# A Mamba-attention-MoE block on one core: first attention group fed from SBUF, pairwise maxima, warm-up products and a shorter spread of side work

## The chip, the core and the metric

The kernel runs on one core of one Trainium2 chip. Its time is device time in microseconds; the time before is the median of three runs. Engines are named as in the profile: PE is TensorE (matrix products), DVE VectorE, ACT ScalarE, POOL GpSimd, SP the engine that issues most transfers.

## The reference, cut to what matters

```python
x = L0_attn_x                                  # (8, 512, 256)
xn = _layernorm(x, axis=-1)
x = x + _L0_attn_ref(xn, ...) + _L0_ffn_ref(xn, ...)

# _L0_attn_ref: projection, causal convolution over 4 rows, a linear state-space scan
# with 16 states, silu, output projection
u = x @ W_in + b_in
u = conv(u, conv_w) + conv_b
h = At @ h + u_t * Bp ; y_t = Cp . h + Dp * u_t
return silu(y) @ W_out + b_out

# _L0_ffn_ref: attention of 16 heads of width 16, and a mixture of 8 experts, top 2
qkv = (x @ W_qkv + b_qkv).reshape(B, S, 3, H, hd)
attn = softmax(q k^T / sqrt(hd)) @ v
gate = softmax(x @ W_gate + b_gate); top_g, top_i = top_k(gate, 2)
moe_out = sum over the two experts of gate * (x @ W_experts[e] + b_experts[e])
return attn_out + moe_out
```

## The kernel before

Rows of one batch (512) lie in four tiles of 128. Attention runs in 32 groups: 8 batches times 4 groups of four heads. A group `i` has eight steps `s`, each one tile `t` of 128 rows times one pair `pr` of heads (`t, pr = divmod(s, 2)`), so there are 256 steps in all. A step number in the text counts them: step 8 i + s.

For each half `h` of a batch's heads, `project_ops` makes queries (w = 0) and keys (w = 1): PE multiplies (`on_pe`, 16 instructions through `mm2`, line 132), ACT rounds the result to the fast matrix format (`upper`, line 1397), DVE makes the remainder (`lower`, line 1402), and SP stores both parts to DRAM (`store`, line 1413). `load_stack` then fills `qs` and `ks` for one group with 16 transfers of 64 KB issued by SP (line 1434), in which the parts are repeated so that one product holds the sum over parts.

A group then goes through `maxima` (PE, line 1443) and `reduce_max` (DVE, line 1455), once for each of the eight steps; `place_parts` (DVE), `place_turn` (PE) and `place_row` (ACT) turn the maxima into a row `mrow`; `weights` (PE, lines 1479 and 1487) makes scores less maximum, `exponent` (ACT, line 1497) the exponentials, `values` (PE, line 1506) multiplies with the values, and `norm_evict`, `norm_turn`, `norm_scale`, `norm_add` divide by the sums and add to `acc` on POOL (line 1537).

Side work goes on between these steps: `gates_of` (layer norm, transposes, gates), `v_of` (values), `scan_setup` (the scan as a convolution kernel), `route_ops` and `scatter_ops` (routing; POOL writes rows by index, line 1076), `ssm_ops` (scan `ps_zx`, projection `ps_z` line 1279, convolution on DVE line 1294, output `ps_o` line 1317), `moe_ops` (36 blocks of 256 rows, products `ps_e`, result to `y_d`), and `combine_ops` (POOL gathers two expert rows per token, 64 gathers at line 1157, and adds them, line 1167).

The order of all instructions comes from a planner in the kernel itself. `op(engine, us, at, fn, needs, makes, takes, frees, ...)` enters an operation with its assumed cost and a due time `at` in steps. `plan` is a greedy list scheduler: on each engine it takes the operation that can start first, or among those within 0.2 us the one that is marked `first` or due earliest. `takes` and `frees` name buffers with a number of copies (`rings`); PSUM has three pairs `m` and one single `m1`. `run_all` makes six plans and emits the shortest by the planner's own count. Each engine then runs its instructions in that fixed order, so one instruction that waits holds up all behind it on the same engine. `needs` like `reach(at)` only order the plan; on the chip only the data and the buffers are waited for.

The due times of the side work come from `spread`, which lays the sum `SIDE` of its costs evenly over the steps from -`LEAD` to the last step:

```python
    def spread(ws):
        for w in ws:
            total[0] += w
            yield -LEAD + (NK - 1 + LEAD) * (total[0] - w / 2) / SIDE
```

with `NK` = 256 and `LEAD` = 6. Transfers that are not needed at once (`later`: W_in, W_out, the biases) are planned after the stack of group 1.

## Time and profile before

| what | before |
|---|---|
| median of three runs | 826.58 us (825.75 to 827.12) |
| profiled execution | 856.68 us |
| its span | 855.0 us |
| PE busy | 761.3 us, 89% |
| DVE busy | 558.9 us, 65% |
| ACT busy | 477.4 us, 56% |
| POOL busy | 387.8 us, 45% |
| moved by DMA | 148.69 MB, 174 GB/s |
| granted PE clock, mean | 0.963 |

The times of single instructions all come from the one profiled execution, which took 30 us longer than the median; its sum is compared with 856.68, not with 826.58. A row of the profile names the line of the kernel, the engine, what is written and read, how often, busy time and the mean of one, and in brackets or behind the bar how long the engine stood idle before it and what ended the wait. "issue" is time for which the profile shows no cause. A row of the windows gives busy time in a stretch for each engine, the number of instructions, the granted PE clock, and the share of the DMA engines. In the chain by time each line is a piece of the chain that ended last: start, length, what.

### The profile page before, as it was taken

To read this page: it belongs to the slowest core of one execution; us is meant where nothing else is said; L and a number is where in the kernel's file an instruction comes from. 1 tells how busy PE (TensorE), PEld (TensorE's weight loads), DVE (VectorE), ACT (ScalarE), POOL (GpSimd) and SP (SyncE) were. 2 spreads that over 40 slices of the span, in tenths; PEclk is the share of its full clock that TensorE was granted. 3 is DMA by queue.
4 is the path that set the end of the run, shared out by engine and by line. 5 is a ranking of instruction groups with operands and counts; after the bars stand their busy time and mean duration, and the time that the engine had idled before them with its cause. 6 is when DMAs were issued, how large, how long until landed. Compare 5 with 4: busy or idle time off the path is not lost.

```text
span 855.0 us, 15265 instructions
## 1 busy us (share of the span) xinstructions
PE 761.3 (89%) x5788; PEld 452.5 (53%) x5788; DVE 558.9 (65%) x852; ACT 477.4 (56%) x652; POOL 387.8 (45%) x419
## 2 busy tenths in 40 slices
PE   4887888988787888999999999999999979897996
PEld 3643454644344445467666676666566645453543
DVE  2466777799773474973547874534885636956884
ACT  2345677444874476854655755665664645535552
POOL 4001011797656755453323322322222145888884
PEclk9998999998988899999999999999999999998999
DMA  6567777332673545477877674897565772969231
GB/s 140 174 178 207 206 221 202 121 75 73 209 205 131 190 131 173 139 209 248 205 212 241 172 226 143 252 234 219 143 172 162 216 191 75 242 177 221 78 108 38
DMA packets 110412, 148.69 MB, mean 174 GB/s; under 512 B 33883, under 2 KB 70787, under 8 KB 110340
## 3 DMA queue, kind: packets, MB, share of 16 engines
q1 hardware_dynamic: 94212, 96.33, 41.0%
q0 software_dynamic: 16128, 51.39, 20.4%
q8 instruction: 46, 0.75, 0.4%
q14 instruction: 26, 0.21, 0.1%
HBM read 96.28 MB, written 51.38 MB: 173 GB/s over the span
## 4 chain that ended last, share of the span: by engine, by line
PE 53%; POOL 16%; DVE 12%; ACT 7%; issue 6%; DMA 4%; another core or an unknown queue 1%; SPq 1%; POOLq 0%; ACTq 0%; DVEq 0%
PE av L1506 8%; PE ps_e L132 8%; POOL got L1157 7%; PE ps_qk L132 6%; DVE mx L1455 5%; PE ps_mx L1443 5%; PE ps_p L1479 5%; PE ps_o L1317 5%; POOL res L1167 5%; PE ps_z L1279 4%; PE ps_p L1487 4%; ACT p L1497 4%; PE ps_zx L132 2%; PE ps_v L132 2%; POOL acc L1167 2%
## 5 line engine op out<-in xcount | busy, mean ns | idle before, releaser
L1455 DVE TENSOR_REDUCE mx<-ps_mx 128x2 f32<-128x1024 f32 x256 | 312.0, 1220 | 166.1 <-PE ps_mx L1443 131.8
L1497 ACT ACTIVATE p<-ps_p 128x1024 f32<-128x1024 f32 x256 | 257.6, 1023 | 117.6 <-PE ps_p L1487 89.2
L1443 PE MATMUL ps_mx<-ks,qs 64*128 64x512 f32 x512 | 126.2, 483 | 23.6 <-DVE mx L1455 19.6
L1479 PE MATMUL ps_p<-qs,ks 64*128 64x512 f32 x512 | 125.1, 483 | 18.5 <-ACT p L1497 11.5
L1506 PE MATMUL av<-p,v_aug 128*32 128x512 f32 x1024 | 127.4, 608 | 0.5 <-issue 0.4
L1487 PE MATMUL ps_p<-mrow,pick 64*128 64x512 f32 x512 | 106.7, 411 | 0.2 <-ACT mrow L1473 0.2
L1443 PEld LDWEIGHTS ps_mx<-ks,qs 64*128 64x128 f32 x512 | 51.4, 190 | 90.9 <-DVE mx L1455 37.4
L1479 PEld LDWEIGHTS ps_p<-qs,ks 64*128 64x128 f32 x512 | 51.1, 195 | 82.3 <-ACT p L1497 28.2
L1111 POOL DMA_DIRECT2D xg<-xs_d x36 | 47.2, 1311 | 95.3 <-PE ps_xg L137 40.8
L1537 POOL TENSOR_TENSOR acc<-acc,attn 128x256 f32<-128x256 f32 x32 | 24.9, 778 | 141.3 <-DVE attn L1530 126.3
L1076 POOL DMA_INDIRECT xs_d<-xs,slot x64 | 65.9, 1030 | 49.2 <-ACT xs L1092 34.1
L1294 DVE SCALAR_TENSOR_TENSOR ys<-th,cw,ys 128x511 f32<-128x511 f32 (+2 forms) x96 | 78.4, 816 | 1.7
L1157 POOL DMA_INDIRECT got<-y_d,slot x64 | 64.8, 1013 | 25.0 <-issue 15.3
L132 PE MATMUL ps_e<-wt,xgT 64*128 64x256 f32 x576 | 69.6, 381 | 1.1 <-DMA wt<-in_L_ffn_W_experts_dram,wrow 0.4
L1279 PE MATMUL ps_z<-zx,wi 128*128 128x512 f32 x128 | 65.7, 637 | 2.7 <-DVE acc L1327 2.1
L1116 POOL DMA_INDIRECT wt<-in_L_ffn_W_experts_dram,wrow x36 | 36.4, 1012 | 68.3 <-PE ps_mx L1443 29.8
L1317 PE MATMUL ps_o<-wo,ys 128*128 128x256 f32 x256 | 62.8, 388 | 1.5 <-DVE ys L1308 1.5
L132 PEld LDWEIGHTS ps_e<-wt,xgT 64*128 64x128 f32 x576 | 54.3, 186 | 12.2 <-ACT xgT L1130 4.8
L1506 PEld LDWEIGHTS av<-p,v_aug 128*32 128x32 f32 x1024 | 27.4, 110 | 57.5 <-issue 56.1
L1487 PEld LDWEIGHTS ps_p<-mrow,pick 64*128 64x128 f32 x512 | 52.2, 198 | 5.8 <-issue 0.4
L1317 PEld LDWEIGHTS ps_o<-wo,ys 128*128 128x128 f32 x256 | 47.5, 195 | 7.6 <-DVE ys L1308 2.3
L132 PE MATMUL ps_qk<-xnTr,wqkv_sb 64*128 64x256 f32 x384 | 46.3, 381 | 2.9 <-ACT p L1497 2.8
(188 smaller groups left out, 963.8 us busy)
## 6 DMA issues: line engine op xcount, KB each, us to landing
split<-parts SPq DMA_DIRECT2D x32, 512.0 KB
qs<-split SPq DMA_DIRECT2D x256, 64.0 KB
ks<-split SPq DMA_DIRECT2D x256, 64.0 KB
xg<-xs_d POOLq DMA_DIRECT2D x36, 256.0 KB
y_d<-y SPq DMA_DIRECT2D x36, 256.0 KB
xn_d<-xn SPq DMA_DIRECT2D x32, 128.0 KB
acc<-in_L_attn_x_dram SPq DMA_DIRECT2D x8, 512.0 KB
xnr<-xn_d SPq DMA_DIRECT2D x16, 256.0 KB
```

The costliest lines, as they stand in the source:

```text
L132: mm(o, lhsT=lhs, rhs=rhs, start=(j == 0), stop=(j == len(parts) - 1))
L1076: nc.gpsimd.indirect_dma_start(out=xs_views[view], out_offset=bass.IndirectOffsetOnAxis(ap=index, axis=0), in_=src, in_offset=None,)
L1157: nc.gpsimd.indirect_dma_start(out=got[b, h][:, t, i, :], out_offset=None, in_=y_d[:, :], in_offset=bass.IndirectOffsetOnAxis(ap=slot[:, i ...
L1279: mm(held["z", b, ct], lhsT=wi[:, c, ct * P : (ct + 1) * P], rhs=zx[b][:, c, :], start=(c == 0), stop=(c == ND - 1),)
L1294: nc.vector.scalar_tensor_tensor(y[:, lag:S], held["th", b, ct][:, 0 : S - lag], cw[:, ct, k : k + 1], bias_tab[:, ct, :] if lag == 0 else ...
L1317: mm(o, lhsT=ys[b][:, ct, t * P : (t + 1) * P], rhs=wo[:, ct, :], start=False, stop=(ct == NCT - 1),)
L1443: mm(ps[:, u, :], lhsT=qs[i % 3][64 * u : 64 * u + 64, pr, t * P : (t + 1) * P], rhs=ks[i % 3][64 * u : 64 * u + 64, pr, :], start=True, s ...
L1455: nc.vector.tensor_reduce(mx[i][:, t, 2 * pr : 2 * pr + 2], held["x", i, s], AX.X, ALU.max, negate=True)
L1479: mm(ps[:, u, :], lhsT=ks[i % 3][64 * u : 64 * u + 64, pr, t * P : (t + 1) * P], rhs=qs[i % 3][64 * u : 64 * u + 64, pr, :], start=True, s ...
L1487: mm(ps[:, u, :], lhsT=pick[64 * u : 64 * u + 64, pr, :], rhs=held["mrow", i][64 * u : 64 * u + 64, :], start=False, stop=True,)
L1497: nc.scalar.activation(p, held["s", i, s], AF.Exp, scale=SCALE)
L1506: mm(av[i][j * HW : (j + 1) * HW, :], lhsT=v_aug[b % 2][:, t, o : o + HW], rhs=pm[i, 2 * t + j // 2][:, j % 2, :], start=(t == 0), stop=(t ...
```

## The change

Four edits are made together.

1. For group 0 alone, `qs` and `ks` are filled from the parts in SBUF (`load_first_stack`) rather than from their copy in DRAM, in 32 transfers of 32 KB, one set of 16 for each pair of heads and w: queries issued by SP, keys by ACT (`nc.scalar`). The store of these parts is planned 8 steps later.
2. For group 0 the steps are taken by pairs: first the four with pair 0 (`s` = 0, 2, 4, 6), then those with pair 1. `place_parts`, `place_turn` and `place_row` run once for each pair, into an `mrow` of their own.
3. `warm` puts 40 products of the identity matrix with itself on PE ahead of everything else.
4. `spread` lays the side work over steps up to 250 instead of 255 (`EARLY` = 5).

As the planner makes all orders anew, the instructions of every engine are ordered differently from there on.

```diff
--- before.py
+++ after.py
@@ -560,6 +560,15 @@
     op("pool", 0.8, -4, set_flip, makes=["flip"])
 
 
+
+    def warm():
+        ps = pair("ps_warm")
+        for n in range(40):
+            mm(ps[:, n % 2, 0:P], lhsT=ident, rhs=ident, start=True, stop=True)
+
+    op("pe", 4.0, -99, warm, takes=[("m", "warm")], frees=[("m", "warm")], shape=3)
+
+
     toep = const.tile([P, S], F32, name="toep")
     bias_tab = const.tile([P, NCT, S], F32, name="bias_tab")
     kpad = dram.tile([1, P + S], F32, name="kpad")
@@ -1418,22 +1427,29 @@
         at = 16 * h - 24
         fast = h == 0
         for w in range(2):
-            M, T, R = ("m", "qk", h, w), ("parts", h, w), ("split" + str(w), h)
-            op("pe", 1.75, at, lambda w=w: on_pe(w), needs=xT_keys(b) + ["wqk"], makes=[("qk", h, w)], takes=[M, T, R], frees=[("xnT", b)])
+            M, T, R = ("m", "qk", h, w), ("parts", h, w), [("split" + str(w), h)]
+            op("pe", 1.75, at, lambda w=w: on_pe(w), needs=xT_keys(b) + ["wqk"], makes=[("qk", h, w)], takes=[M, T] + R, frees=[("xnT", b)])
             op("act", 0.69, at, lambda w=w: upper(w), needs=[("qk", h, w), "bqk"], makes=[("up", h, w)], first=True)
             op("dve", 0.75, at, lambda w=w: lower(w), needs=[("up", h, w)], makes=[("lo", h, w)], frees=[M], first=fast)
-            op("sp", 0.4, at + 0.5, lambda w=w: store(w), needs=[("lo", h, w)], makes=[("split", h, w)], frees=[T], kb=512)
+            op("sp", 0.4, at + 0.5 + 8 * fast, lambda w=w: store(w), needs=[("lo", h, w)], makes=[("split", h, w)], frees=[T], kb=512)
 
     def load_stack(i, w):
         st = (qs, ks)[w][i % 3]
-        src = split_of[i // 2, w]
         for u in range(2):
             for r in range(4):
                 part = (r // 2, r % 2)[w]
-                rows = src[part, 4 * HD * (i % 2) : 4 * HD * (i % 2 + 1), :]
-                nc.sync.dma_start(
-                    out=st[64 * u + HD * r : 64 * u + HD * (r + 1), :, :].bitcast(F32),
-                    in_=rows.rearrange("(pr u d) s -> u d pr s", u=2, d=HD)[u],
+                to = st[64 * u + HD * r : 64 * u + HD * (r + 1), :, :].bitcast(F32)
+                rows = split_of[i // 2, w][part, 4 * HD * (i % 2) : 4 * HD * (i % 2 + 1), :]
+                nc.sync.dma_start(out=to, in_=rows.rearrange("(pr u d) s -> u d pr s", u=2, d=HD)[u])
+
+    def load_first_stack(w, pr):
+
+        for u in range(2):
+            for r in range(4):
+                o = (2 * pr + u) * HD
+                (nc.sync, nc.scalar)[w].dma_start(
+                    out=(qs, ks)[w][0][64 * u + HD * r : 64 * u + HD * (r + 1), pr, :].bitcast(F32),
+                    in_=held["pt", 0, w][o : o + HD, (r // 2, r % 2)[w], :].bitcast(F32),
                 )
 
     def maxima(i, s):
@@ -1456,10 +1472,10 @@
             mx[i][:, t, 2 * pr : 2 * pr + 2], held["x", i, s], AX.X, ALU.max, negate=True
         )
 
-    def place_parts(i):
+    def place_parts(i, pairs=slice(0, 2)):
         v = negm[i % 2].rearrange("p t (u c) -> p t u c", u=2)[:, :, :, 0:4]
-        v = v.rearrange("p t u (r z) -> p t u r z", z=2)
-        m = mx[i].rearrange("p t (r u) -> p t u r", u=2)
+        v = v.rearrange("p t u (r z) -> p t u r z", z=2)[:, :, :, pairs]
+        m = mx[i].rearrange("p t (r u) -> p t u r", u=2)[:, :, :, pairs]
         nc.vector.tensor_copy(v[:, :, :, :, 0], m)
         nc.vector.tensor_tensor(v[:, :, :, :, 1], m, v[:, :, :, :, 0].bitcast(F32), ALU.subtract)
 
@@ -1468,9 +1484,11 @@
             f"ps_nm_{i}", [lambda r, t=t: negm[i % 2][r, t, :].bitcast(F32) for t in range(NT)]
         )
 
-    def place_row(i):
-        held["mrow", i] = wk2.tile([P, S], F32R, tag="mrow", name=f"mrow_{i}")
-        nc.scalar.copy(blocks(held["mrow", i]), held["nm", i])
+    def place_row(i, pairs=(0, 1)):
+        row = wk2.tile([P, S], F32R, tag="mrow", name=f"mrow_{i}_{pairs[0]}")
+        nc.scalar.copy(blocks(row), held["nm", i])
+        for pr in pairs:
+            held["mrow", i, pr] = row
 
     def weights(i, s):
         t, pr = divmod(s, 2)
@@ -1487,7 +1505,7 @@
             mm(
                 ps[:, u, :],
                 lhsT=pick[64 * u : 64 * u + 64, pr, :],
-                rhs=held["mrow", i][64 * u : 64 * u + 64, :],
+                rhs=held["mrow", i, pr][64 * u : 64 * u + 64, :],
                 start=False,
                 stop=True,
             )
@@ -1543,36 +1561,65 @@
         K = 8 * i
         Q = [("stack0", i), ("stack1", i)]
         for w in range(2):
+            if i == 0:
+                for pr in range(2):
+                    op(
+                        ("sp", "act")[w], 3.3, K - 16 + 0.1 * w + pr, lambda w=w, pr=pr: load_first_stack(w, pr),
+                        needs=[("lo", 0, w)], makes=[("stack0", w, pr)] + ([("stack", 0, w)] if pr else []),
+                        takes=[] if pr else [("stack" + str(w), 0)], frees=[("parts", 0, w)], kb=256, first=w > 0,
+                    )
+                continue
             op(
                 "sp", 3.6, K - 16 + 0.1 * w, lambda w=w: load_stack(i, w),
                 needs=[("split", i // 2, w), ("split", i // 2, w + i % 2 * (1 - w))], makes=[("stack", i, w)],
                 takes=[("stack" + str(w), i)], frees=[("split" + str(w), i // 2)], kb=512,
             )
-        for s in range(8):
-            k = K + s
-            X = ("m", "mx", i, s)
+
+        turns = ([0, 2, 4, 6], [1, 3, 5, 7]) if i == 0 else (list(range(8)),)
+        n = 0
+        for half, steps in enumerate(turns):
+            for s in steps:
+                k = K + n
+                n += 1
+                X = ("m", "mx", i, s)
+                op(
+                    "pe", 0.24, k - 10, lambda s=s: maxima(i, s), needs=([("stack", i, 0), ("stack", i, 1)] if i else [("stack0", 0, half), ("stack0", 1, half)]) + (reach(k - 18) if i != 1 else [("nm", 0)]),
+                    makes=[("mp", i, s)], takes=[X, ("mx_m", i, s)], first=i == 0,
+                )
+                op(
+                    "dve", 1.23, k - 10, lambda s=s: reduce_max(i, s),
+                    needs=[("mp", i, s)] + ([("mr", i, 0)] if s else []),
+                    makes=[("mr", i, s)], takes=[] if s else [("mx", i)], frees=[X, ("mx_m", i, s)], first=True,
+                )
+            at = K - 2.5 if i else k - 9.5
+            end = half == len(turns) - 1
+            some = slice(half, half + 1) if i == 0 else slice(0, 2)
+            N, R = ("nm", i, half), ("mrow", i, half)
             op(
-                "pe", 0.24, k - 10, lambda s=s: maxima(i, s), needs=[("stack", i, 0), ("stack", i, 1)] + (reach(k - 18) if i != 1 else [("nm", 0)]),
-                makes=[("mp", i, s)], takes=[X, ("mx_m", i, s)],
+                "dve", 0.37, at, lambda some=some: place_parts(i, some), needs=[("mr", i, s) for s in steps] + [("negm0", i % 2)] + ([("nmp", i, 0)] if half else []),
+                makes=[N] + ([("nm", i)] if end else []), takes=[] if half else [("negm", i)], frees=[("mx", i)], first=True,
             )
             op(
-                "dve", 1.23, k - 10, lambda s=s: reduce_max(i, s),
-                needs=[("mp", i, s)] + ([("mr", i, 0)] if s else []),
-                makes=[("mr", i, s)], takes=[] if s else [("mx", i)], frees=[X, ("mx_m", i, s)], first=True,
-            )
-        op(
-            "dve", 0.37, K - 2.5, lambda: place_parts(i), needs=[("mr", i, s) for s in range(8)] + [("negm0", i % 2)],
-            makes=[("nm", i)], takes=[("negm", i)], frees=[("mx", i)], first=True,
-        )
-        op("pe", 0.45, K - 2.5, lambda: place_turn(i), needs=[("nm", i)], makes=[("nmp", i)], takes=[("mt", "nm", i), ("mrow", i)], frees=[("negm", i)])
-        op("act", 0.58, K - 2.5, lambda: place_row(i), needs=[("nmp", i)], makes=[("max", i)], frees=[("mt", "nm", i)], first=True)
-        for s in range(8):
-            k = K + s
+                "pe", 0.45, at, lambda: place_turn(i), needs=[N], makes=[("nmp", i, half)],
+                takes=[("mt", "nm", i, half), R], frees=[("negm", i)], first=i == 0,
+            )
             op(
-                "pe", 0.47, k, lambda s=s: weights(i, s), needs=[("max", i), "pick"], makes=[("wp", i, s)],
-                takes=[("m", "p", i, s), ("p_m", i, s)], frees=Q + [("mrow", i)],
-            )
-            op("act", 1.04, k, lambda s=s: exponent(i, s), needs=[("wp", i, s)], makes=[("p", i, s)], takes=[("p", i, s)], frees=[("m", "p", i, s), ("p_m", i, s)], first=True)
+                "act", 0.58, at, lambda half=half: place_row(i, (half,) if i == 0 else (0, 1)), needs=[("nmp", i, half)],
+                makes=[("max", i, half)] + ([("max", i)] if end else []), frees=[("mt", "nm", i, half)], first=True,
+            )
+        n = 0
+        for half, steps in enumerate(turns):
+            for s in steps:
+                k = K + n
+                n += 1
+                op(
+                    "pe", 0.47, k, lambda s=s: weights(i, s), needs=[("max", i, half), "pick"], makes=[("wp", i, s)],
+                    takes=[("m", "p", i, s), ("p_m", i, s)], frees=Q + [("mrow", i, half)],
+                )
+                op(
+                    "act", 1.04, k, lambda s=s: exponent(i, s), needs=[("wp", i, s)], makes=[("p", i, s)],
+                    takes=[("p", i, s)], frees=[("m", "p", i, s), ("p_m", i, s)], first=True,
+                )
         for hf in range(2):
             vs = [("vd", b, n) for n in range(2)]
             four = [("p", i, s) for s in range(4 * hf, 4 * hf + 4)]
@@ -1605,14 +1652,14 @@
 
     rings["split0"] = rings["split1"] = 2
     NK = B * NG * 8
-    LEAD = 6.0
+    LEAD, EARLY = 6.0, 5.0
     total = [0.0]
 
     def spread(ws):
 
         for w in ws:
             total[0] += w
-            yield -LEAD + (NK - 1 + LEAD) * (total[0] - w / 2) / SIDE
+            yield -LEAD + (NK - 1 - EARLY + LEAD) * (total[0] - w / 2) / SIDE
 
     SSM = [3.9] + [1.75] * 4 + [1.87] * 4 + [0.0]
     SCAN = [0.2] + [0.6] * 9 + [1.0, 1.0, 2.3]
```

## The prediction, made before the changed kernel was run

> **What bounds the kernel now.** I read the page first (busy shares, then the chain that ended last), then the windows, which cut the run into its stages, then the chain by time at the end of the run, and last the timeline of the first 52 us, where most of the edits lie.
>
> ```profile
> span 855.0 us, 15265 instructions
> PE 761.3 (89%) x5788; PEld 452.5 (53%) x5788; DVE 558.9 (65%) x852; ACT 477.4 (56%) x652; POOL 387.8 (45%) x419
> ```
>
> TensorE is busy 89% of the span, so only its idle time (about 94 us) and its slow-clock time can be won. The windows say where these lie:
>
> ```profile
> core 0: us, PE busy (x) PEld busy (x) DVE busy (x) ACT busy (x) POOL busy (x), PEclk, DMA share, GB/s
> 20.00:36.00 16.00, 14.97 (x198) 11.82 (x194) 4.22 (x13) 8.37 (x17) 1.47 (x3) 1.00 0.54 161
> 36.00:51.00 15.00, 10.84 (x66) 7.40 (x62) 11.61 (x15) 1.75 (x3) 0.00 (x0) 0.77 0.84 230
> 380.00:690.00 310.00, 304.77 (x2513) 198.57 (x2513) 184.52 (x249) 178.03 (x238) 84.76 (x79) 1.00 0.72 204
> 735.00:798.00 63.00, 53.41 (x336) 28.08 (x332) 45.17 (x62) 29.82 (x38) 53.71 (x60) 0.92 0.78 204
> 798.00:833.00 35.00, 34.84 (x222) 18.94 (x222) 27.89 (x39) 17.40 (x23) 29.98 (x33) 1.00 0.28 85
> ```
>
> From 380 to 690 PE has 5 us idle in 310: whatever is late there moves the end by the same amount. From 735 to 798 it lacks 9.6 us, and from 798 to 833 almost nothing. Before 36 us it is well filled as well (1.0 us idle in 20 to 36): while the first stack is fetched, PE does the second half's projections and the values of two batches.
>
> ```profile
> 681.32 1.75 PE ps_e L132 x16
> 683.75 5.13 DMA y_d<-y
> 689.15 0.97 POOL got L1157
> ...
> 701.90 9.89 issue
> ...
> 843.64 1.85 issue
> 845.50 0.70 DVE acc L1327
> ```
>
> The end hangs on the last expert product (683), then on a POOL chain of 64 gathers and 64 additions, with a hole of 9.9 us in it, and on PE, whose ps_o ends at 845.4 too. Both tie; cutting one alone gives little.
>
> ```profile
> 13.87 6.52 PE L132 MATMUL ps_qk<-xnT,wqkv_sb 64*128 64x256 f32 x32 [0.68 <-ACT xnT L798]
> 17.71 0.43 DVE L728 BATCH_NORM_STATS2 st<-x 128x6 f32<-128x256 f32 x1 [9.03 <-DMA x<-in_L_attn_x_dram]
> 22.42 4.73 SPq L1434 DMA_DIRECT2D qs<-split  x8
> 23.37 0.59 ACT L892 COPY v_aug<-ps_v 128x512 f32<-128x512 f32 x1 [1.38 <-PE ps_gt L137]
> 36.08 1.15 PE L1443 MATMUL ps_mx<-ks,qs 64*128 64x512 f32 x6
> ```
>
> Here is what the first stack costs now: parts ready at 19.55 and 21.91 (DVE's `lower`), stored, loaded from 22.4 to 30.9 in 16 issues on SP, first maxima at 36.08. From 36 to 51 DVE's eight reductions of 1.22 us set the pace and PE is thin.
>
> **Part 1, identity products (PE, 40 of 128x128).** They run from about 1.5 us (the identity is made by POOL at 1.23 + 0.29) beside the row loads; PE has nothing before 11.77. What they may win is in the row at 13.87: 32 products take 6.52 us where two such sets took 1.89 and 1.95 from 24.99 on, so 2.7 us. The Trainium skill ("TensorE: Matmul & The Clock Gate", What's actually happening) says the clock is halved until PE has been busy for one window of about 3.4 us, which fits, although the window's row shows 1.00 at that time. The same section says that one idle window halves it again, and this speaks against the edit: 40 products at 0.1 to 0.2 us end by 6 to 9.5, before 11.77. By the rule the win is 0 to 2.7 us of PE. I cost it at nothing for another reason, the row at 17.71: `lower` of the queries stands on DVE behind the statistics of batch 1, which wait for a load that lands at 17.7, and the changed DVE order keeps that. `lower` ends at 19.55 and 21.5 instead of 19.55 and 21.91. If the cover were gone it would be 2.7 us.
>
> **Part 2, first stack from SBUF, keys issued by ACT.** Removed from the way to it: the store and the load through DRAM. A DMA issue on SP costs 0.47 us (4 of 8 rows at 0.42 plus 0.047 between). Eight for the query pair 0 run on SP from 19.6 to 23.3, eight for the keys on ACT from 21.5 to 25.3, landing 2.0 us later (a load of 8 KB issued at 12.23 is used at 14.26): first maxima at 27.5, 8.5 us earlier. No row shows a DMA issued by ACT. I take SP's 0.47; the smallest row on SP is 0.22 (be_raw, one row each), so 16 issues cost ACT 3.5 to 7.5 us. The skill ("DMA: Bandwidth & Descriptors", Issuing engines are not separate DMA queues) has the two queues share the same DMA engines and save issue time alone. That is 3.7 us here; the rest of the 8.5 is the DRAM round trip.
> What is queued behind: on ACT both evictions of `ps_v`, then the four normalizations of batch 1 (now 23.4 to 27.5). In the changed order all 16 key issues come first, and the order's waits show that DMAs reuse eight completion semaphores among SP and ACT: the tenth key issue waits for the store of the key parts (512 KB, issued at about 24.2; the query store took 19.58 to 23.9 until the load behind it could go). So ACT comes free at about 28.5 + 7 x 0.47 = 31.8. The second maxima needs the PSUM pair of `ps_v`, so it starts at 32.4, the transposes of batch 1 (after two evictions and 2.1 us of normalization) at 34.5, the gate, the second half's query projection and the rest after that. PE idles from 23.7 to 27.5 and is thin until about 37, and the clock halves, as it did at 40 to 47 now.
> SP: 8 more issues sit between the stores and the second stack, and four stores of normalized rows wait for ACT, so the second stack lands at about 43 instead of 41; it is needed at 50, so this costs nothing. The projection stores of the second half wait for parts that are now made 17 us later; stack 2 lands at about 67 to 69, when it is needed.
>
> **Part 3, maxima by pairs.** Added: two small DVE operations (2 x 0.18), four transposes (0.45), one copy (0.58); 1.4 us in all, off PE but for 0.45. Won: step 0 needs four reductions instead of eight, 4.9 us.
>
> **Front, summed.** I count PE's work in the two instruction orders, each group by its back-to-back row (1.75 for a projection, 0.43 for two 512-wide products, 1.75 for four value pairs, 3.9 for a scan). At step 0 the old order has done 26.9 us, the new one 18.5; at step 8 42.7 and 41.8; at step 16 61.5 and 60.9; at the last expert product 631.3 and 630.9. Step 0 now starts at 50.7, so 23.8 us are lost by then. In the new one, from 34.5 on: gate 1.1, projection 1.75, four more reductions 4.9, place and turn 1.5, second projection 1.75 and maxima between, some at half clock: step 0 at about 48, 29.5 lost. So the first exponentials come some 3 us earlier, with 8 us less work done. Between steps 8 and 16 the old order lets DVE stand 3.5 us for the load of batch 3 (its statistics come after four of eight reductions); the new one puts six before. I give back 3. Front: +3 us (ACT at 0.22 each and no semaphore wait: -5; ACT held longer: +10).
>
> **Part 4, side work five steps shorter.** The order shows what moves: the last batch's scan from step 242 to 236, its first ps_z from 245 to 241, the output products of batch 6 from 243 to 239. Steps 220 to 240 now hold 51.1 us of PE work and will hold 60.6; steps 240 to 250 fall from 32.9 to 23.4. The former ran from 735 to 798 with 9.6 us idle and 5 us lost at half clock; the latter is the full stretch. About half of the moved 9.5 us should fit into waits: -5. The last ps_o waits 1.5 us for DVE (838.65 to 841); with ps_z one step earlier: -1. On POOL the hole of 9.9 goes: attention addition 25 (ready at 711.7) stood ahead of the third group of gathers and now stands behind the fourth, 26 us after the first gather rather than 13. POOL alone would end 10 us earlier, so it no longer ties with PE; worth nothing by itself. Tail: -6 (0 to -10).
>
> **Sum.** 856.7 (span 855.0 and 1.7 around it) + 3 - 6 = 853.7. The reordering of everything between steps 16 and 203 shifts single waits (11 PE gaps of 1.0 to 5.7 us in its timeline there, 22 us in all): 0, with +-4. The median of the runs is 826.6, 3.5% under the profiled execution; I scale the change by 0.965: 823.7 us.
>
> **Rivals.**
> ACT is held too long (slower). Place: the 16 key issues; price: 1 us per us, as transposes, gates and projections are behind them. If the stores take the 6.4 us that one took at 65 and each further semaphore round 2 us more, ACT is free at 38 or later: +10 - 6 = +4, 830.5. It decides from 35 us on, where the sum is zero. For it: PSUM has only three pairs; against: the DMA share of 0.54 leaves room. 0.22.
> The tail gives nothing (slower). ACT stood 6.2 us at 694 to 700 and 4.6 at 775 to 780, each while POOL issued eight gathers in a row. The new order has such a pair in batch 6 instead of batch 4, in the last 50 us, where work was to be fitted in. +3, 829.5; it decides when less than 3 of the 6 arrives. 0.15.
> The front works as meant: ACT issues at 0.22, the store is not waited for: -5 - 6 = -11, 816. For it: first maxima 8.5 us earlier; against: PE had other work then. 0.18.
> The change does nothing in sum, as PE work is the same (777 us): 0.05.
> The sum as written: 0.40.
>
> **The numbers.** Predicted 823.7; its own case spans 819 to 828. The range over the cases is 811 to 835. About 0.2% (1.65 us) is what the measurement tells from no change. Faster: 0.30 of the 0.40 and the 0.18: 0.48. Same: 0.07 of the 0.40 and the 0.05: 0.12. Slower: the two rivals and 0.03: 0.40.
>
> **What would show it.** Right: first maxima at 27 to 28; ACT's first `ps_v` eviction at 31 to 33; first exponential at 47 to 50; step 16 at 93 to 96 (91.7 now); no POOL wait over 3 us after the gathers begin; PE idle between steps 220 and 240 under 6 us. Wrong: the eviction before 27 or after 35; POOL still ending with PE; the last expert product more than 8 us from 683.

## The result, and the profile after

The changed kernel is slower: 833.99 us (median of seven, 829.14 to 840.60) against 826.17 us for the kernel before, a ratio of 1.0093 with a 95% interval of 1.0064 to 1.0122. The forecast was 823.7. The time lies inside the range given, on the other side of no change.

To read the numbers: in some comparisons the kernel before takes about 826 us, in others about 858, and the kernels beside it move with it (some expectations below speak of two chips, but the record has chip 14 at both levels, so the reason is not known); ratios are therefore taken within one comparison, and stages compared between profiles of one level. The profile of before shown above (856.68) and its later repeats are of the 858 level, the profile after (829.14, span 827.4) is of the 826 level. There the kernel with the shorter spread alone (ratio 1.0013 to the kernel before) stands in for the kernel before, which has no profile at that level.

The busy shares of after, and its windows (columns as before):

```profile
span 827.4 us, 15473 instructions
PE 755.2 (91%) x5864; PEld 455.5 (55%) x5864; DVE 555.4 (67%) x854; ACT 475.3 (57%) x653; POOL 391.4 (47%) x419
```

```profile
20.00:36.00 16.00, 7.45 (x38) 5.07 (x39) 4.74 (x10) 2.60 (x6) 1.47 (x3) 0.66 0.45 125
36.00:51.00 15.00, 12.67 (x112) 8.78 (x112) 9.01 (x13) 5.59 (x10) 0.00 (x0) 0.79 0.52 144
380.00:690.00 310.00, 303.48 (x2502) 194.88 (x2498) 183.65 (x246) 178.23 (x240) 94.54 (x91) 1.00 0.72 204
735.00:798.00 63.00, 60.34 (x397) 29.89 (x396) 53.10 (x72) 35.17 (x45) 53.41 (x56) 1.00 0.55 149
```

PE was busy 14.97 of the 16 us from 20 to 36; now it is busy 7.45, at a granted clock of 0.66. The stretch from 380 to 690 is as full as before, so nothing lost ahead of it is made up there. From 735 to 798 the 9.6 us of idle have become 2.7. As the changed kernel is at other steps by then, the same count by steps is safer: from step 220 to 240 PE was idle 9.6 us (8.7 in a later profile) and is now idle 2.8 (4.3 in the second profile), as forecast. The timeline of after, in order of start (start, length, engine, what; in brackets the wait before it):

```profile
1.58 10.71 PE L567 MATMUL ps_warm<-ident 128*128 128x128 f32 x80 [1.58 <-POOL ident masks.py:199]
13.61 3.73 PE L132 MATMUL ps_qk<-xnT,wqkv_sb 64*128 64x256 f32 x32 [0.68 <-ACT xnT L807]
22.33 11.03 ACTq L1450 DMA_DIRECT2D ks<-parts  x15
25.47 6.89 SPq L1450 DMA_DIRECT2D qs<-parts  x8
25.85 0.46 PE L1459 MATMUL ps_mx<-ks,qs 64*128 64x512 f32 x1
30.17 0.76 PE L1459 MATMUL ps_mx<-ks,qs 64*128 64x512 f32 x1 [3.86 <-DMA qs<-parts]
33.40 1.08 ACT L901 COPY v_aug<-ps_v 128x512 f32<-128x512 f32 x2 [14.47 <-DMA ks<-parts]
36.00 1.50 PE L137 MATMUL ps_xT<-ident,xn 64*128 64x64 f32 x16 [1.16 <-ACT xn L754]
48.57 1.02 ACT L1515 ACTIVATE p<-ps_p 128x1024 f32<-128x1024 f32 x1
```

ACT issues keys from 22.33 to 33.36 and does nothing else. What is queued behind, the value evictions, waits until 33.40; PE's maxima need the PSUM pair that they free, and the transposes of batch 1 come at 36.00. The forecast said 31.8 for the end of the issues, 31 to 33 for the eviction, 34.5 for the transposes, and about 48 for step 0. The last part of the chain that ended last is this:

```profile
817.16 0.73 POOL acc L1555
817.89 0.02 issue
817.91 0.70 DVE acc L1336
818.61 0.04 issue
818.65 0.39 PE ps_o L1324
819.04 1.73 PE ps_o L1326 x8
```

POOL's addition releases DVE's, which frees the PSUM pair that PE's last output product needs: in this profile POOL sets the end, and PE waits 2.5 us for it. In the second profile of the same kernel the chain runs through PE, DVE and ACT without POOL from 804 us on, and POOL's last attention addition is itself the one that waits, 4.6 us, for DVE. So the two still tie.

### The profile page after: what moved, and what is told of

The parts are those of the page before. It is cut to its first block, busy times and chain, and to the rows that moved or that the text cites. A ratio compares the mean times of both kernels' runs of the same rounds, so it can differ in the third digit from the quotient of the medians.

```text
span 827.4 us, 15473 instructions
## 1 busy us (share of the span) xinstructions
PE 755.2 (91%) x5864; PEld 455.5 (55%) x5864; DVE 555.4 (67%) x854; ACT 475.3 (57%) x653; POOL 391.4 (47%) x419
## 3 DMA queue, kind: packets, MB, share of 16 engines
q0 software_dynamic: 16128, 51.39, 21.1%
## 4 chain that ended last, share of the span: by engine, by line
PE 51%; DVE 17%; ACT 8%; POOL 7%; DMA 7%; issue 4%; SPq 3%; ACTq 1%; DVEq 0%; POOLq 0%
PE av L1524 8%; PE ps_e L132 7%; DVE mx L1471 7%; PE ps_mx L1459 5%; PE ps_p L1497 5%; PE ps_o L1326 5%; PE ps_qk L132 5%; POOL got L1166 4%; PE ps_p L1505 4%; ACT p L1515 3%; PE ps_z L1288 3%; DVE ys L1303 3%; ACT xs L1101 3%; PE ps_zx L132 2%; DMA got<-y_d,slot 2%
## 5 line engine op out<-in xcount | busy, mean ns | idle before, releaser
L1459 PE MATMUL ps_mx<-ks,qs 64*128 64x512 f32 x512 | 126.0, 478 | 30.9 <-DVE mx L1471 18.0
L1524 PE MATMUL av<-p,v_aug 128*32 128x512 f32 x1024 | 123.5, 600 | 0.0
L1505 PE MATMUL ps_p<-mrow,pick 64*128 64x512 f32 x512 | 104.0, 400 | 0.0
L1459 PEld LDWEIGHTS ps_mx<-ks,qs 64*128 64x128 f32 x512 | 51.1, 189 | 93.5 <-DVE mx L1471 33.9
L1497 PEld LDWEIGHTS ps_p<-qs,ks 64*128 64x128 f32 x512 | 49.9, 189 | 72.9 <-ACT p L1515 25.4
L1166 POOL DMA_INDIRECT got<-y_d,slot x64 | 67.0, 1046 | 24.8 <-issue 14.9
L1326 PE MATMUL ps_o<-wo,ys 128*128 128x256 f32 x256 | 60.4, 379 | 0.0
L132 PE MATMUL ps_qk<-xnTr,wqkv_sb 64*128 64x256 f32 x384 | 49.9, 402 | 3.2 <-ACT p L1515 2.3
```

The costliest lines, as they stand in the source:

```text
L132: mm(o, lhsT=lhs, rhs=rhs, start=(j == 0), stop=(j == len(parts) - 1))
L1166: nc.gpsimd.indirect_dma_start(out=got[b, h][:, t, i, :], out_offset=None, in_=y_d[:, :], in_offset=bass.IndirectOffsetOnAxis(ap=slot[:, i ...
L1326: mm(o, lhsT=ys[b][:, ct, t * P : (t + 1) * P], rhs=wo[:, ct, :], start=False, stop=(ct == NCT - 1),)
L1459: mm(ps[:, u, :], lhsT=qs[i % 3][64 * u : 64 * u + 64, pr, t * P : (t + 1) * P], rhs=ks[i % 3][64 * u : 64 * u + 64, pr, :], start=True, s ...
L1497: mm(ps[:, u, :], lhsT=ks[i % 3][64 * u : 64 * u + 64, pr, t * P : (t + 1) * P], rhs=qs[i % 3][64 * u : 64 * u + 64, pr, :], start=True, s ...
L1505: mm(ps[:, u, :], lhsT=pick[64 * u : 64 * u + 64, pr, :], rhs=held["mrow", i, pr][64 * u : 64 * u + 64, :], start=False, stop=True,)
```

## The experiments

The edits are cut to the lines that matter; lines that only tell the planner the same thing (engine names, keys) are left out. Three theories stood at the start. Theory 1: the front costs (the stack from SBUF, with ACT held), and the loss lasts, as PE is full later. Theory 2: the shorter spread brings nothing or costs. Theory 3: any change makes the planner re-make the order of every engine, and that alone moves the time by several us. "Ratio" is to the kernel before in the same comparison, with its 95% interval. Single executions of one kernel spread by about 1% to either side (the kernel before: 852.11 to 865.07 in 22 runs), so ratios of medians decide and one profile is good for some 5 us.

A measure used below is the time lost at a step: the moment when the step's first exponential starts, minus the PE work that stands ahead of it in PE's instruction order, counted with the same durations as in the prediction. At the end it is the span minus all PE work (777 us). The counted durations are a little too long, so the figure falls where PE is full; only differences between kernels at one level mean something.

| time lost, us, at step | 0 | 8 | 16 | 40 | 80 | 208 | end |
|---|---|---|---|---|---|---|---|
| before (858 level) | 24.8 | 26.9 | 29.8 | 31.0 | 70.5 | 47.4 | 77.2 |
| before + 8 issues on ACT | 29.3 | 31.4 | 33.8 | 34.7 | 72.9 | 51.7 | 76.3 |
| before + 16 issues on ACT | 34.5 | 36.7 | 36.8 | 38.1 | 78.5 | 59.6 | 88.3 |
| before + pairs | 21.4 | 27.1 | 32.5 | 37.8 | 82.5 | 62.2 | 93.8 |
| before + spread (826 level, as all below) | 23.3 | 27.3 | 28.9 | 27.9 | 44.0 | 21.1 | 45.2 |
| after | 30.1 | 32.8 | 33.8 | 33.9 | 55.4 | 35.0 | 50.0 |
| after, second profile | 31.2 | 34.1 | 35.1 | 38.2 | 60.5 | 40.1 | 58.4 |
| after, stack through DRAM | 19.8 | 25.1 | 29.6 | 29.3 | 43.1 | 32.1 | 46.2 |
| after, keys issued by POOL | 21.4 | 29.8 | 30.5 | 31.7 | 56.1 | 34.8 | 51.8 |
| after, keys of pair 1 later | 28.4 | 27.8 | 30.8 | 32.7 | 50.9 | 30.0 | 45.4 |

**Both kernels again.** No edit.

> The kernel before, unchanged: a second profiled execution of it, and how far two sets of runs of one kernel lie apart. All theories: ratio 1.000 within 0.3%. If its profiled span is near 825 and the 380 to 690 stretch ends some 25 to 30 us earlier than in the first profile, the first profile held a disturbance after 260 us and the comparison of stages has to be made with this one.

Measured: 1.0017 (0.9994 to 1.0040), as expected. The profile (span 860.7) is as long as the first one of before (855.0), so that length was no accident of one execution.

> The changed kernel, unchanged, beside the parts below on one chip. Expected: 0.5 to 1.2% slower than the kernel before, as in the first comparison. If it is faster than before by the tail term alone (-0.4% or better), the first comparison turned on the chip.

Measured: 1.0074 (1.0045 to 1.0102), 831.84 against 825.95. The loss repeats.

**One part alone in the kernel before.** First the 40 products:

```diff
+    op("pe", 4.0, -99, warm, takes=[("m", "warm")], frees=[("m", "warm")], shape=3)
```

> Only the 40 identity products are added to the kernel before. If the front is what costs (theory 1: SBUF stack with ACT holding up the second projection) this alone is 0, 825 to 828 us, with the first query projection at 3.7 us instead of 6.5. If any new order of the plan moves the time by several us (theory 3), this, which re-makes the whole order, lies anywhere between 820 and 836.

Measured: 1.0000 (0.9973 to 1.0026). Nothing, as forecast. It doesn't speak against theory 3, as the expectation has it: in the traces PE, POOL and SP run exactly the order of before, and DVE and ACT differ from it in one place each. The planner made the same order again. Then the spread, twice:

```diff
-            yield -LEAD + (NK - 1 + LEAD) * (total[0] - w / 2) / SIDE
+            yield -LEAD + (NK - 1 - 5.0 + LEAD) * (total[0] - w / 2) / SIDE
```

> Only the side work is spread over five steps less. Prediction's term: -5 to -6 us, 820 to 822. Theory 2 (the spread gives nothing, or costs because the same work is squeezed between steps that were full): 826 to 834. Theory 1 (the front is the cost): at or under 826.

> Only the spread of five steps less, once more. If the tail term holds on both chips: 0.993 to 0.998. If it was a matter of the slower chip, whose end is longer: 0.999 to 1.003.

Measured: 0.9964 (0.9940 to 0.9988) at the 858 level, 1.0013 (0.9999 to 1.0026) at the 826 level: -3 and +1 us, where the prediction's sum had -6. Theory 2 holds for this part taken alone. The steps that were to be filled were filled: PE's idle time from step 220 to 240 fell from 9.6 and 8.7 us to 4.6 and 4.5. But from step 250 to the end it rose from 6.9 to 14.7 in both runs. The timeline of the second shows why; PE is early and waits for POOL:

```profile
809.72 0.72 POOL L1537 TENSOR_TENSOR acc<-acc,attn 128x256 f32<-128x256 f32 x1
810.47 0.69 DVE L1327 TENSOR_TENSOR acc<-ps_o,acc 128x512 f32<-128x512 f32 x1 [9.49 <-POOL acc L1537]
811.22 0.58 PE L1315 MATMUL ps_o<-be,combT 128*128 128x256 f32 x1 [9.27 <-DVE acc L1327]
```

Then the pairs alone (stack through DRAM, no identity products, spread to step 255):

```diff
-        for s in range(8):
+        turns = ([0, 2, 4, 6], [1, 3, 5, 7]) if i == 0 else (list(range(8)),)
+        for half, steps in enumerate(turns):
+            for s in steps:
```

> The kernel before with group 0 taken by pairs alone (stack through DRAM, no identity products, spread to step 255). First exponential at about 44 instead of 52 (-4.9 for four reductions, +1.4 for small operations, and less). PE has the same work, so by step 16 most of that is given back: ratio 0.997 to 1.003. If any new order moves the time by itself: outside of that.

Measured: 1.0156 (1.0107 to 1.0205), 13 us slower: outside of what was expected, and the sign named for theory 3. (Here the order really is another one: PE's departs from that of before within its first 300 instructions.) The first exponential does come 8 us earlier (43.6), but with 5 us less PE work done; at step 8 the time lost equals that of before, and then it grows: +2.7 at step 16, +6.8 at 40, +12 at 80. In that stretch its granted clock is lower. Its window, then those of two profiles of the kernel before at the same level:

```profile
92.00:158.00 66.00, 58.06 (x571) 30.27 (x569) 47.17 (x92) 43.92 (x70) 7.50 (x15) 0.89 0.68 186
```

```profile
92.00:158.00 66.00, 58.33 (x572) 32.42 (x572) 49.32 (x100) 45.16 (x69) 14.85 (x21) 1.00 0.72 198
92.00:158.00 66.00, 58.33 (x550) 32.01 (x551) 46.78 (x95) 43.19 (x66) 11.77 (x19) 0.95 0.72 199
```

PE is equally busy, at 0.89 instead of 1.00 or 0.95: 58 us times 0.06 to 0.11 is 3.5 to 6.4 us of work not done. Over all its executions the mean clock is 0.952 against 0.959 in the kernel before. What in the order makes the clock fall was not found.

**One part taken out of the changed kernel.** The stack through DRAM, with pairs, products and spread kept (group 0 then goes the way of all groups, through `load_stack`):

```diff
-            op("sp", 0.4, at + 0.5 + 8 * fast, lambda w=w: store(w), needs=[("lo", h, w)], makes=[("split", h, w)], frees=[T], kb=512)
+            op("sp", 0.4, at + 0.5, lambda w=w: store(w), needs=[("lo", h, w)], makes=[("split", h, w)], frees=[T], kb=512)
...
-            if i == 0:
+            if False:
                 for pr in range(2):
```

> The changed kernel with the first stack stored to DRAM and loaded from it by SP, as in the kernel before; pairs, identity products and shorter spread kept. If the stack from SBUF is the cost of the front (ACT held, PE idle 20 to 36): this has PE busy 15 of the 16 us from 20 to 36 again and lies at or under the spread alone, 0.3 to 0.6% faster than the kernel before. If the pairs are the cost: it stays 0.5% or more slower than the kernel before.

Measured: 0.9999 (0.9979 to 1.0018), 824.92 us. PE has its work back in the stretch:

```profile
20.00:36.00 16.00, 14.51 (x170) 11.74 (x168) 5.57 (x17) 7.16 (x14) 1.47 (x3) 1.00 0.60 170
```

So in the presence of the other edits the stack from SBUF, with the order that the planner makes for it, costs 831.84 - 824.92 = 6.9 us, which is all of the loss; the pairs, the products and the spread together are worth nothing at the end. They are not worth nothing on the way: at step 208 this version has lost 11.0 us more than the spread alone (32.1 against 21.1), and makes it up behind that step. Then the pairs taken out:

```diff
-        turns = ([0, 2, 4, 6], [1, 3, 5, 7]) if i == 0 else (list(range(8)),)
+        turns = (list(range(8)),)
```

> The changed kernel with all eight maxima of group 0 before one placing, as in the kernel before; stack still from SBUF. The prediction put the pairs at -3.5 us at step 0 and near nothing in work done: time within 0.3% of the changed kernel. If the pairs cost (the 1.4 us of small operations and the transposes that stand in line on PE at half clock): 2 to 4 us faster than it.

Measured: 1.0138 (1.0117 to 1.0160), 5 us slower than the changed kernel: a miss. With the stack late, all eight reductions now stand ahead of step 0:

```profile
44.03 1.23 DVE L1471 TENSOR_REDUCE mx<-ps_mx 128x2 f32<-128x1024 f32 x1 [21.55 <-PE ps_gt L137]
```

DVE stands 21.6 us before the first of them, and the first exponential comes at 62.0 instead of 49.7. Given the late stack, the pairs are what softens it. Last the spread taken out, twice:

```diff
-    LEAD, EARLY = 6.0, 5.0
+    LEAD, EARLY = 6.0, 0.0
```

> The changed kernel with the spread as in the kernel before (last step 255 instead of 250): all of the front, nothing of the tail. Theory 1 (front costs about +3 and more): 829 to 836. Theory 2 (the tail is the cost): back to 824 to 828. With the prediction's own numbers (front +3, tail -6): slower than the changed kernel by 6, about 840.

> The changed kernel with the spread to step 255 once more, beside the next[...]. If the tail term holds on both: 1.012 to 1.018, that is 4 to 8 us above the changed kernel.

Measured: 1.0167 (1.0114 to 1.0220) and 1.0221 (1.0199 to 1.0243), 6 to 12 us slower than the changed kernel, whose ratio is 1.0074 to 1.0093. So the spread, worth nothing alone, is worth about the forecast 6 us, or more, inside the changed kernel. In the second run PE's idle time from step 250 to the end is 17.9 us, 13.1 of it one wait for POOL, where the changed kernel has 7.5; in the first run it is 8.0, so this isn't the whole of it. PE's orders show one thing that goes with it: up to the last expert product they hold 631 us of PE work before, 640 with the pairs, and 631 again with pairs and spread.

**ACT's hold by itself.** The kernel before, with ACT issuing 8 or 16 transfers ahead of its first value eviction, into a stack that is not yet in use. Nothing reads what they bring, and in the traces every engine keeps the order of before, so theory 3 has no part in this experiment.

```diff
         def evict(half):
+            if b == 0 and half == 0:
+                for n in range(16):
+                    o = 16 * (n % 8)
+                    nc.scalar.dma_start(
+                        out=ks[2][o : o + 16, n // 8, :].bitcast(F32),
+                        in_=held["pt", 0, 1][o : o + 16, n % 2, :].bitcast(F32),
+                    )
```

> The kernel before, unchanged, for a profile beside the next three. Ratio 1.000 within 0.3%. If the end is bound by POOL (gathers and additions after the last expert product): 165 to 172 us from the last expert product to the end, and an idle stretch of PE of 3 us or more before the last two ps_o.

> The kernel before, with 8 transfers of 32 KB (key parts in SBUF to the not yet used third key stack) issued by ACT ahead of its first value eviction; nothing reads what they bring, and every other instruction keeps its place. ACT is held for 8 x 0.65 = 5.2 us. Hold theory: PE loses about 3 us around 24 to 32, and the time rises by 2 to 4 us (0.25 to 0.5%). If the hold is hidden (only the later stack costs): within 0.15%.

> As the run with 8, with 16 issues: ACT is held for about 11 us, to 33. Hold theory: PE idle in 20 to 36 rises from 1 us to 8 or 9, and the time rises by 5 to 9 us (0.6 to 1.1%), all of the loss. If less than half of that comes, the rest of the changed kernel's loss is in its order and its stack.

Measured: 1.0022 (0.9983 to 1.0061) for the kernel before; 1.0029 (1.0003 to 1.0056) with 8; 1.0050 (1.0026 to 1.0075) with 16: 2.5 and 4.3 us. As the unchanged kernel itself came out at 1.0022, the 2.5 us can't be told from nothing; the 4.3 us (2.2 to 6.4) are clear of no change. The profile of the unchanged kernel missed both signs of an end bound by POOL: it has 174.3 us from the last expert product to the end (165 to 172 were expected), and PE is nowhere idle over 1.1 us in its last 24 us. So POOL and PE tie in the kernel before, as the prediction said. The first eviction in the timelines with 0, 8 and 16 issues:

```profile
23.27 0.59 ACT L892 COPY v_aug<-ps_v 128x512 f32<-128x512 f32 x1 [1.38 <-PE ps_gt L137]
```

```profile
21.02 6.01 ACTq L895 DMA_DIRECT2D ks<-parts  x7
27.08 0.59 ACT L899 COPY v_aug<-ps_v 128x512 f32<-128x512 f32 x1 [6.28 <-DMA ks<-parts]
```

```profile
21.71 11.13 ACTq L895 DMA_DIRECT2D ks<-parts  x15
32.89 0.59 ACT L899 COPY v_aug<-ps_v 128x512 f32<-128x512 f32 x1 [11.40 <-DMA ks<-parts]
```

```profile
20.00:36.00 16.00, 6.77 (x86) 5.45 (x78) 2.29 (x8) 4.25 (x10) 1.47 (x3) 0.77 0.51 152
```

The last line is the window with 16 issues: PE 9.2 us idle, where the changed kernel has 8.6. The eviction slips by 3.8 and 9.6 us, the first exponential by 4.6 and 9.8 (51.74, 56.26, 61.48). That is the hold, as theory 1 has it; with 16 issues a little under half of the slip reaches the end. It is a little under the 5 us that was the least expected, and about two thirds of the 6.9 us that the stack from SBUF costs. The table shows the slip shrink from 9.8 at step 8 to 7.1 at step 40; the single profiles are too far apart after that to follow it.

**Other engines and other places for the key loads.** All three start from the changed kernel, and in all three the planner makes a largely new order, which the result includes. Behind the value evictions, for pair 1:

```diff
-                        ("sp", "act")[w], 3.3, K - 16 + 0.1 * w + pr, lambda w=w, pr=pr: load_first_stack(w, pr),
+                        ("sp", "act")[w], (3.3, 5.2)[w], K - 16 + 0.1 * w + pr * (1 + 6 * w), lambda w=w, pr=pr: load_first_stack(w, pr),
-                        takes=[] if pr else [("stack" + str(w), 0)], frees=[("parts", 0, w)], kb=256, first=w > 0,
+                        takes=[] if pr else [("stack" + str(w), 0)], frees=[("parts", 0, w)], kb=256, first=w > 0 and pr == 0,
```

> The changed kernel with the key loads of pair 1 placed behind ACT's two value evictions of batch 0; ACT still issues all 16. Hold theory: the evictions come at about 28 instead of 33 to 34, but the four normalizations of batch 1 still stand behind the second eight issues (until 34), so half of the cost or less comes back: ratio 1.003 to 1.006. If the hold does not matter: unchanged, 1.007 to 1.009.

Measured: 0.9974 (0.9957 to 0.9991), 823.53 us. The eviction came at 28.58 as expected; more came back than expected, 8 to 10 us against the changed kernel. This version beats both kernels, by 2.1 us against the one before. What came back isn't PE's idle time of that stretch:

```profile
20.00:36.00 16.00, 6.61 (x44) 4.41 (x44) 6.26 (x13) 3.40 (x8) 1.48 (x3) 0.76 0.53 146
```

PE is idle 9.4 us here, as in the changed kernel (8.6), and ACT's normalizations come at 33.99, hardly sooner than its 34.36. But DVE is busy 6.26 us instead of 4.74: as the evictions come sooner, DVE has its first three reductions done at 34.72 instead of 39.31, and the first exponential comes at 45.58 instead of 48.57. How much of the gain is the new order was not tested. On POOL:

```diff
-                (nc.sync, nc.scalar)[w].dma_start(
+                (nc.sync, nc.gpsimd)[w].dma_start(
```

> The changed kernel with the 16 key loads issued by POOL, which has 1.5 us of work between 20 and 36, instead of ACT. The stack still comes from SBUF and about as late. If the hold of ACT is the cost (11 us for 15 issues): first value eviction at 23 to 25, PE idle between 20 and 36 under 4 us instead of 10, and the time falls by 5 to 7 us against the changed kernel (ratio to before 0.999 to 1.002). If it is the late stack itself, whoever issues it: first maxima near 30, step 0 at 48 or later, ratio 1.005 to 1.010.

Measured: 1.0058 (1.0036 to 1.0080). First eviction at 22.42 and PE idle 4.5 us from 20 to 36, so the hold is gone; first maxima at 31.00, step 0 at 43.5. At step 16 the time lost is 30.5, near the 29.6 of the kernel with the stack through DRAM; from step 40 to 80 it grows by 24.4 us where that one has 13.8. The hold theory's figure (0.999 to 1.002) missed; the early gain was lost later. As the intervals of this version and of the changed kernel overlap, taking the hold off ACT isn't shown to help by itself: the late stack, the issues on POOL and the new order stay as rivals. On SP, behind the queries:

```diff
-                (nc.sync, nc.scalar)[w].dma_start(
+                nc.sync.dma_start(
```

> The changed kernel with the 16 key loads of the first stack issued by SP instead of ACT. If the hold of ACT until 33 us is what costs (the prediction's first rival): the first value eviction at 24 to 26 instead of 33.4, PE idle between 20 and 36 falls from 8.5 to under 4 us, and the time falls by 4 to 8 us (about 0.5 to 1%). If SP becomes the hold instead (16 more issues of 0.47 us ahead of the second stack): first maxima near 31, time within 0.3% of the changed kernel. If any new order moves the time (theory 3): anything within 1%.

Measured: 1.0205 (1.0180 to 1.0230), the slowest of all. The eviction came at 24.18, but now SP is the hold:

```profile
24.74 10.88 SPq L1450 DMA_DIRECT2D ks<-parts  x16
36.80 5.97 SPq L1450 DMA_DIRECT2D qs<-parts  x8
50.79 4.22 SPq L1443 DMA_DIRECT2D ks<-split  x8
```

The second pair's queries are issued at 36.80 and the second group's keys end at 55.0, so step 8 starts at 80.2 (75.9 in the changed kernel). The expected range for this case (within 0.3%) was too small.

**The place of the last expert product.** A spread of 2.5 steps in the kernel before moves it from 631 to 637 us of PE work; one of 12 steps in the best version moves it from 627 to 624.

> The kernel before with the spread 2.5 steps shorter (0 and 5 both measured near 1.000). By PE's order the last expert product has 636.9 us of PE work up to it, where it has 631.3 with 0 and 631.7 with 5. If the place of that product sets the end: 5 us later there and 3 to 6 us in the time, ratio 1.004 to 1.007. If the spread works by its amount: between the two, 0.997 to 1.001.

> The version with the keys of pair 1 behind the value evictions (0.9974), with the spread 12 steps shorter: 624.3 us of PE work up to the last expert product instead of 627.0. POOL then ends some 3 us earlier, but in that version PE had no idle stretch left at its end, so PE bounds: 0.994 to 0.998 if it gains at all. If more side work ahead of step 244 crowds the DVE stage (steps 48 to 80): 1.000 or more.

Measured: 0.9992 (0.9967 to 1.0018) and 1.0108 (1.0056 to 1.0159). The place alone does not decide: in the first, the gathers begin 3 us later than before (691.4 against 688.2), but the POOL chain to its last attention addition takes 154.5 us instead of 158.9. The second missed too: its loss appears from step 40 to 56, where the time lost goes from 30.9 to 49.6. Why the spread is worth so much in the changed kernel, and nothing without the other edits, stays open.

## Why the prediction was wrong

The sum was +3 for the front, 0 for everything from step 16 to 203, and -6 for the tail. The step that failed is the 0 in the middle: 9 to 13 us were lost there. The front was put 1 to 3 us too small. The tail did shrink by the forecast amount or more, though not for the reason given.

**Identity products: worth nothing, as forecast, but longer than forecast.** They took 10.71 us in 80 instructions of 0.134, not 4 to 8, and so reach to the transposes at 12.22. No idle window is left, and the 32 products at 13.61 take 3.73 instead of 6.52, the 2.7 us that were named as the most. (What an idle window would have done to the clock, the rule weighed there, these runs therefore don't show.) It is worth nothing because DVE's statistics wait for batch 1 (until 18.54), the cover that the prediction named.

**Front, +3: right in kind, too small.** Forecast: 29.5 us lost at step 0 against 23.8, then 3 given back. Measured by the same count: 30.1 and 31.2 in the two profiles. At step 16 they have lost 33.8 and 35.1, the kernel before 29.8 (other level) and the spread alone 28.9: +4 to +6 rather than +3. The end of ACT's issues, 33.4 against 31.8, is near by luck, as two errors offset each other. An issue from SBUF took 0.60 us plus 0.045 between, on ACT and on SP, not the 0.47 taken from DRAM loads: 2.8 us more for 16. And the tenth issue's wait for the store, until 28.5 in the forecast, doesn't show: three of the 15 issues took 0.82, 1.03 and 1.44 us, the others 0.51 to 0.60. First maxima came in two halves (25.85 and 30.17) around the forecast 27.5. The first rival, that ACT is held too long, was right in place; its price of 1 us per us was about double, as 9.8 us of slip cost 4.3.

**Re-ordering from step 16 to 203 taken as 0, with 4 either way: the step that failed.** At step 208 the changed kernel has lost 13.9 and 19.0 us more than the spread alone at the same level (35.0 and 40.1 against 21.1). Of this, 4.9 and 6.2 stood at step 16, so 9.0 and 12.8 were added where the prediction had nothing. Most of it comes from step 16 to 80: 21.6 and 25.4 us lost there, 15.1 with the spread alone, 13.5 in the changed kernel with the stack through DRAM. The pairs, which were to be free by step 16, have their share: alone they have lost 14.8 us more than the kernel before at step 208, and cost 13 us at the end. The error was to end the account at step 16. Whether the later steps suffer from the thin front itself or from the order that the planner makes for it was not separated.

**Tail, -6: it came, but the mechanism was wrong.** From step 208 to the end the changed kernel loses 15.0 and 18.3 us, the spread alone 24.1, the kernel before 29.8 (other level). Steps 220 to 240 were filled as described (PE idle 2.8 and 4.3 us), and taking the spread out costs 6 to 12 us. So the tail gave back part of what the middle had lost; how much of that is the spread's doing, and how much comes from a PE that arrives late, was not separated. But "POOL alone would end 10 us earlier, so it no longer ties with PE" was wrong. In all traces but one POOL's last attention addition ends 148 to 160 us after its first gather, and 5.6 to 12.4 us remain from there. PE work moved ahead of step 240 leads only to a wait where PE is early: with the spread alone PE stands 9.3 us for POOL at the end, and the gain is -3.1 and +1.1 us. In the changed kernel, where PE is late, that wait is 2.5 us in one profile and 0.4 in the other, and POOL still ends with PE, which the prediction had named as a sign of being wrong. So the second rival (the tail gives nothing) is right for the spread alone and not for this kernel.

**Signs and chances.** Most signs named for "right" came true: first exponential at 48.57, step 16 at 94.7, the eviction at 33.4 (31 to 33 was named), PE idle 2.8 us between steps 220 and 240. The time went the other way all the same, as none of them lies between step 16 and step 208. 0.40 went to a sum that needed this stretch to be free, and nothing shown spoke for that.

## What to carry to other kernels

Count what stands behind a transfer on the engine that issues it: 16 issues are 10 us in which that engine does nothing else, and the version with half of them behind two short evictions was 1% faster here, new order included. An account of a change at the start has to go on until its effect is shown to be gone: here it grew from 5 or 6 us at step 16 to 14 or 19 at step 208. Where two engines tie at the end, a gain on one of them is zero until the other's chain, from its own last input on, is shown to be shorter. An order made by a planner has interactions: a part worth nothing alone (the spread) and a part that costs alone (the pairs) can cancel, so test parts in and out, not only in.

## What the runs showed of the hardware

- A transfer of 32 KB from SBUF to SBUF (16 rows) took 0.60 us to issue on ACT and on SP alike; a load of 64 KB from DRAM 0.42 on SP; the same 32 KB issued by POOL 0.52 with what lies between (11 in 5.68 us). Of ACT's 15 issues in a row in the second profile of after, only two were over 0.9 us (1.09 and 1.40); what held these two was not found, and it cost little more than 1 us.
- From 92 to 158 us PE was busy 58.1 to 58.3 us in three profiles, and was granted a clock of 0.89 in one (pairs alone) and of 0.95 and 1.00 in the others (the kernel before), though PE had no idle gap over 0.9 us in that stretch of the first.
